# An RWKV-6 block on one core: the last group's recurrence and back part divided by time instead of by channels and sequences

## The chip, the cores and the metric

One core of one Trainium2 chip runs the whole kernel. The metric is the device time of a run in microseconds (us); the time before is the median of three runs, 1524.67 (1521.03 to 1527.92). Engines are called as the profile calls them: PE (matrix products and transposes), PEld (its weight loads), DVE (VectorE), ACT (ScalarE), POOL (GpSimd), SP (issues most DMAs).

## The reference

Input are 32 sequences of 128 tokens with 512 channels (32 heads of 16), a state for each sequence, and the weights of one RWKV-6 layer:

```
xn = ln(x);  sx = token_shift(xn)                       # previous token minus this one
x5 = xn + sx * (maa_stack + tanh((xn + sx*maa_x) @ maa_w1) @ maa_w2)      # five mixes
w = exp(-exp(time_decay + tanh(x5[1] @ decay_w1) @ decay_w2))
r, k, v = x5[3] @ Wr.T, x5[0] @ Wk.T, x5[2] @ Wv.T;  g = silu(x5[4] @ Wg.T)
per sequence and head, token after token, s is 16x16:
    a = k[:, None] * v[None, :];   out = r @ (u * a + s);   s = a + w[:, None] * s
x = x + (groupnorm(out) * g) @ Wo.T
xn2 = ln(x);  xk, xr = two token-shift mixes of xn2
x = x + sigmoid(xr @ ffn_Wr.T) * (relu(xk @ ffn_Wk.T)**2 @ ffn_Wv.T)
```

All is computed in float32.

## The kernel before

**Groups and parts.** The 32 sequences form 8 groups of 4 (512 tokens each). For each group five generators make the instructions: `front_mix` (layer norm, transposes, mixes), `front_proj` (decay, k, r, v), `front_gate` (the gate, parked in DRAM as `dgate`), `prep` (bonus sums and products that make the recurrence step two tokens at a time) and `back` (L810: group norm, gate, output product with `wo`, second layer norm, feed-forward part with `fk`, `fr`, `fv`, store). The recurrence is a row of units that goes through all groups.

**The recurrence.** Partitions are (sequence, head), 128 in all. Tokens are taken in pairs, so a row of time has 64 steps. A group has two passes over the value dimension (`dh`, 8 of 16 columns each), and a pass has 16 units, one for each key row q, and a bonus unit. A unit is:

- ACT: copies the pair decays into a PSUM tile `sc` (L705, two buffers) and the first state column into `a` (L716, two buffers);
- POOL (`rec_pool`): `am = v * k` (L730, 128x1024) and the sum of the two halves of each pair into `a` (L734);
- DVE (`rec_dve`): the scan over time `sc = scan(sc, a)` (L752) and `rm = sc * r` (L754, two buffers);
- PE (`rec_pe`): 8 transposing products that add `rm` into the PSUM tile `acc` (L787, one buffer).

The bonus unit is L761, L764 and L768 on DVE and 8 more products. At the end of a pass ACT copies `acc` into `y` (L801). POOL can be at most two units ahead of the scan, since `a` has two buffers and is freed by the scan.

**The back part.** On `y` of a group: squares on ACT (L829), a sum over each head on DVE (L832), a reciprocal square root in twelve small DVE instructions (L835 to L842), the scaling of `y` (L844); then for each of four channel blocks a PE transpose (L855), gain and bias on ACT (L864), the gate on DVE (L866); the `wo` product (L875) and the residual with a running sum (L884). The second layer norm takes squares on ACT (L354), a small power on POOL (L359) between L357 and L361 on DVE, scaling on ACT (L368), transposes (L394), gain and bias (L384, L895), and two mixes on DVE (L898, L910). Then come the products with `fk` (L408), `fr` (L949) and `fv` (L965), two DVE instructions for the result (L954, L956) and the store (L958). Seven groups do it whole; the last group does it in two streams of two sequences each, both of which begin when the whole recurrence has ended.

**What sets the order.** A planner (`Plan`, with a model of each engine and of the tile buffers) decides while the program is built. Each generator yields operations with an engine, an estimated time, what they read and write and the buffers they take; of those that could start first, it takes the one with the earliest due time. `DUE` holds the due times of each part in units of a group; `last1` and `last2` are the two streams of the last group. The emitted order on each engine is fixed, and each engine works through its own in order.

**Last weights.** `last_weights` (L804) loads `wo`, `fk`, `fr` for the last group into the three weight buffers `wt` as those of group 6 come free, and `fv` when `wo` has been used.

```
            for dh in range(NDH):
                ds = slice(dh * DH, (dh + 1) * DH)
                for q in range(S):
                    (am,) = yield Op(POOL, 2.39, r=[(k, None), (v, None)], w=[(0, None)], alloc=["am"], port=True)
                    nc.gpsimd.tensor_tensor(am.t, v[:, ds, :], k[:, q : q + 1, :].to_broadcast([P, DH, L]), ALU.mult)
```

Of the kernel before, what the change touches and what calls it, by code (L numbers as in the profile page):

```python
# [11 lines left out]
ALU = mybir.AluOpType  # L12
# [36 lines left out]
DUE = {"rec": (0.171, 0.811), "mix": (-4.351, -2.486), "proj": (-6.56, 7.24), "gate": (0.525, 0.545), "prep": (-4.001, 1.375), "back": (-0.209, 3.178), "last1": (-27.722, 1.84), "last2": (7.448, 22.404)}  # L49
# [133 lines left out]
def rwkv6_block(ctx: ExitStack, tc: tile.TileContext, x, prev, s0, vecs, u, maa_w1, maa_w2,  # L183
# [53 lines left out]
    ident = const.tile([P, P], F32, name="ident")  # L237
    mhalf = const.tile([P, GB], F32, name="mhalf")
# [42 lines left out]
    def load_x(g, need=None, bs=range(GB)):  # L281
        b0, b1 = bs[0], bs[-1] + 1
        if g == 0:

            (xt,) = yield Op(SP, 0.4, w=[(0, 0), (0, 1)], alloc=["x"], xfer=2.3)
            nc.sync.dma_start(out=xt[:, 0:2, :], in_=x[0:2].rearrange("b t e -> t b e"))
            yield Op(ACT, 1.4, w=[(xt, 2), (xt, 3)], xfer=2.3)
            nc.scalar.dma_start(out=xt[:, 2:4, :], in_=x[2:4].rearrange("b t e -> t b e"))
            nc.scalar.dma_start(out=vec, in_=vecs)
            nc.scalar.dma_start(out=pv, in_=prev)  # L290
            return xt
        (xt,) = yield Op(SP, 0.4, w=[(0, None)], alloc=["x"], xfer=part(4.5, bs), need=need)
        nc.sync.dma_start(out=xt[:, b0:b1, :], in_=x[g * GB + b0 : g * GB + b1].rearrange("b t e -> t b e"))
        return xt

# [30 lines left out]
    def layernorm_T(g, src, sums, vw, vb, which, use, take, need=None, bs=range(GB)):  # L326
# [35 lines left out]
        for b in bs:  # L362
            if g == 0 and sums is None and b % 2:
# [7 lines left out]
        (xnT,) = yield Op(ACT, 0.25, w=[(0, "p")], alloc=["xnT"], need=need)  # L371
        nc.scalar.copy(xnT[:, :, 0].rearrange("p (e b) -> p e b", b=GB)[:, :, bsl],
                       pv[:, 1 - which, :, g * GB + b0 : g * GB + b0 + nb_])
        late = []

        def evict(e, pt):
            if g == 0 and sums is None:

                yield Op(DVE, 0.69, r=[(pt, None)], w=[(xnT, e)])
                nc.vector.tensor_scalar(xnT[:, e * GB + b0 : e * GB + b0 + nb_, 1 : L + 1], bt(pt[:, cols]),  # L380
                                        col(vw, e), col(vb, e), ALU.mult, ALU.add)
            else:
                yield Op(ACT, part(0.78, bs), r=[(pt, None)], w=[(xnT, e)])
                nc.scalar.activation(xnT[:, e * GB + b0 : e * GB + b0 + nb_, 1 : L + 1], bt(pt[:, cols]), AF.Identity,  # L384
# [16 lines left out]

    def row(xnT, e, shift, bs=range(GB)):

        return xnT[:, e * GB + bs[0] : e * GB + bs[-1] + 1, shift : shift + L]
# [34 lines left out]
    def front_mix(g, d):  # L439
# [8 lines left out]
        def use(xnT, e, pt, tiles):  # L448
# [4 lines left out]
            yield Op(DVE, 0.69, r=[(xnT, e), (xnT, "p"), (pt, None)], w=[(sx, e)])  # L453
# [135 lines left out]
    def prep(g, d):  # L589
# [42 lines left out]
        w01 = yield from pair_decays(w, [w])  # L632
        d.update(st=st, w01=w01)
# [61 lines left out]

    def rec_act(gs):

        for g in gs:
            d = data[g]
            yield Op(ACT, 0.0, need=lambda: "w01" in d and ("v", "all") in d)  # L700
            for dh in range(NDH):
                for q in range(S):
                    sc, = yield Op(ACT, 0.59, r=[(d["w01"], None)], w=[(0, None)], alloc=["sc"])

                    nc.scalar.copy(sc.t, d["w01"][:, q : q + 1, :].to_broadcast([P, DH, T2]))  # L705
# [3 lines left out]
    def rec_state(gs):  # L709
        for g in gs:  # L710
            d = data[g]
            yield Op(ACT, 0.0, need=lambda: "w01" in d and ("v", "all") in d)
            for dh in range(NDH):
                for q in range(S):
                    a, = yield Op(ACT, 0.21, r=[(d["st"], None)], w=[(0, 0)], alloc=["a"])
                    nc.scalar.copy(a[:, :, 0], d["st"][:, q, dh * DH : (dh + 1) * DH])  # L716
                    unit[g, dh, q, "a"] = a
            d["st"].open = False

    def rec_pool(gs):  # L720

        for g in gs:
# [3 lines left out]
            for dh in range(NDH):  # L726
                ds = slice(dh * DH, (dh + 1) * DH)
                for q in range(S):
                    (am,) = yield Op(POOL, 2.39, r=[(k, None), (v, None)], w=[(0, None)], alloc=["am"], port=True)
                    nc.gpsimd.tensor_tensor(am.t, v[:, ds, :], k[:, q : q + 1, :].to_broadcast([P, DH, L]), ALU.mult)  # L730
                    yield Op(POOL, 0.0, need=lambda: (g, dh, q, "a") in unit)
                    a, am2 = unit[g, dh, q, "a"], pair(am.t)
                    yield Op(POOL, 1.03, r=[(am, None)], w=[(a, 1)], port=True, end=[am])
                    nc.gpsimd.tensor_tensor(a[:, :, 1:T2], am2[:, :, 0 : T2 - 1, 0], am2[:, :, 0 : T2 - 1, 1], ALU.add)  # L734
# [3 lines left out]
    def rec_dve(gs):  # L738

        for g in gs:  # L740
# [4 lines left out]
            for dh in range(NDH):  # L745
                ds = slice(dh * DH, (dh + 1) * DH)
                for q in range(S):
# [4 lines left out]
                    nc.vector.tensor_tensor_scan(scf, scf, a.t.rearrange("p d n -> p (d n)"), 0.0, ALU.mult, ALU.add)  # L752
                    (rm,) = yield Op(DVE, 1.21, r=[(sc, None), (r, None)], w=[(0, None)], alloc=["rm"], end=[sc])
                    nc.vector.tensor_tensor(  # L754
                        pair(rm.t), sc.t.unsqueeze(3).to_broadcast([P, DH, T2, 2]),
                        r2[:, q : q + 1, :, :].to_broadcast([P, DH, T2, 2]), ALU.mult)
# [4 lines left out]
                nc.vector.tensor_tensor(rm.t, v[:, ds, :], d["rk"].t.unsqueeze(1).to_broadcast([P, DH, L]), ALU.mult)  # L761
                (am,) = yield Op(DVE, 0.67, r=[(v, None), (d["a10"], None)], w=[(0, None)], alloc=["ps"], port=True)
                bo = am.t.rearrange("p (d n) -> p d n", n=T2)
                nc.vector.tensor_tensor(bo, v2[:, ds, :, 0], d["a10"].t.unsqueeze(1).to_broadcast([P, DH, T2]),  # L764
                                        ALU.mult)
                yield Op(DVE, 0.67, r=[(am, None)], w=[(rm, None)], end=[am])
                rm2 = pair(rm.t)
# [23 lines left out]
    def rec_out(gs):  # L791
        for g in gs:
            d = data[g]
            for dh in range(NDH):
                yield Op(ACT, 0.0, need=lambda: (g, dh, "acc") in unit)
                acc = unit[g, dh, "acc"]
                if dh == 0:
# [6 lines left out]
    def last_weights(W):  # L804

        for name, ap in (("wo", wo), ("fk", fk), ("fr", fr)):
            W[name] = yield from weight(ap, lambda: ("back", "weights") in data[NG - 2])
        W["fv"] = yield from weight(fv, lambda: ("wo", "used") in W)

    def back(g, d, bs=range(GB), W=None):  # L810
# [11 lines left out]
        yield Op(DVE, 0.0, need=lambda: "rec" in d and ("gate", NE - 1) in d)  # L822
        y = d["y"]
        yv = y[:, b0 * H : b1 * H, :]
        n = (b1 - b0) * H
        wot = yield from get("wo", wo, lambda: g < 1 or ("back", "weights") in data[g - 1])
# [199 lines left out]
```

## Time and profile before

The profiled execution took 1523.82 us, with a span of 1522.0 from the first to the last instruction.

| what | value |
|---|---|
| median of three runs | 1524.67 us |
| profiled execution: its time / its span | 1523.82 / 1522.0 us |
| mean granted PE clock | 0.963 |
| PE busy | 1407.3 us (92%) |
| DVE busy | 1264.1 us (83%) |
| POOL busy | 1036.0 us (68%) |
| ACT busy | 652.7 us (43%) |
| DMA moved | 147.04 MB, mean 97 GB/s |

In the profile, busy is the time in which an engine has an instruction under way; `x` behind a tile counts instructions. In a group's line stand the program's names, the shapes, the busy time, the mean duration of one in nanoseconds, and the idle time before them with what ended it. In a timeline each line gives the start, the length and, in brackets, the idle time before it and what ended that. A line of the table by stages gives, for a stretch of the span, each engine's busy time and number of instructions, and last the granted PE clock, the DMA share and GB/s.

### The profile page before, as it was taken

How to read it: one execution, taken by the hardware profiler on the slowest of the kernel's cores; microseconds unless marked ns; L12 is line 12 of the kernel's file. 1: busy time of each engine (PE TensorE's matmuls, PEld its weight loads, DVE VectorE, ACT ScalarE, POOL GpSimd, SP SyncE). 2: the span in 40 equal slices, each digit the busy share in tenths (PEclk: the TensorE clock that was granted, in tenths of full speed). 3: DMA queues.
4: the chain of work that ended last, by engine and by line, in shares of the span. 5: the costliest groups of instructions: out<-in, count | busy, mean ns of one | idle time of the engine just before them, and what ended most of it. 6: DMA issues, size and time to landing. Idle time of an engine off the chain costs nothing.

```text
span 1522.0 us, 16610 instructions
## 1 busy us (share of the span) xinstructions
PE 1407.3 (92%) x5344; PEld 746.5 (49%) x5344; DVE 1264.1 (83%) x1614; ACT 652.7 (43%) x1271; POOL 1036.0 (68%) x642
## 2 busy tenths in 40 slices
PE   5897988889999999999999999999999999689778
PEld 2343454445554555445544555455544555455444
DVE  6539789888998899889988899899988898878732
ACT  3333243324743356423743366423843363344252
POOL 3225884877586959687786959687786959679500
PEclk9897899899999999999999999999999999889989
DMA  6130330424304531244304521244304421400220
GB/s 225 56 87 14 118 103 15 142 82 138 118 24 139 168 102 43 80 143 135 117 31 133 184 86 42 90 143 131 111 32 140 150 98 35 159 28 29 95 71 28
DMA packets 127879, 147.04 MB, mean 97 GB/s; under 512 B 8368, under 2 KB 77616, under 8 KB 126768
## 3 DMA queue, kind: packets, MB, share of 16 engines
q1 hardware_dynamic: 91312, 127.59, 25.4%
q10 hardware_dynamic: 36480, 18.39, 4.2%
q8 instruction: 42, 0.69, 0.2%
q14 instruction: 45, 0.37, 0.1%
HBM read 94.57 MB, written 17.83 MB: 74 GB/s over the span
## 4 chain that ended last, share of the span: by engine, by line
PE 51%; DVE 21%; POOL 18%; issue 5%; ACT 3%; DMA 2%; SPq 0%; POOLq 0%; DVEq 0%; ACTq 0%
PE ps L408 18%; POOL am L730 10%; PE acc L787 8%; PE ps L965 6%; POOL a L734 6%; PE ps L949 6%; PE ps L427 5%; DVE sc L752 4%; DVE rm L754 3%; PE ps L875 2%; PE ps L414 2%; PE ps L465 2%; DVE rk L668 1%; DVE ps L660 1%; POOL mx L488 1%
## 5 line engine op out<-in xcount | busy, mean ns | idle before, releaser
L730 POOL TENSOR_TENSOR am<-v,k 128x1024 f32<-128x1024 f32 x256 | 609.0, 2379 | 34.2 <-DMA r<-blk 15.6
L408 PE MATMUL ps<-mx,wt 128*128 128x512 f32 (+1 forms) x1312 | 585.0, 593 | 17.8 <-DVE mx L456 6.6
L734 POOL TENSOR_TENSOR a<-am 128x504 f32<-128x504 f32 x256 | 286.5, 1119 | 209.4 <-DVE sc L752 183.2
L408 PEld LDWEIGHTS ps<-mx,wt 128*128 128x128 f32 x1312 | 243.8, 194 | 287.4 <-issue 261.9
L752 DVE TENSOR_TENSOR_SCAN sc<-sc,a 128x512 f32<-128x512 f32 x256 | 313.4, 1224 | 35.4 <-POOL a L734 32.3
L754 DVE TENSOR_TENSOR rm<-sc,r 128x1024 f32<-128x1024 f32 x256 | 312.8, 1222 | 32.3 <-PE acc L787 17.1
L787 PE MATMUL acc<-by_head,rm 128*128 128x128 f32 x2176 | 291.5, 284 | 39.1 <-DVE rm L754 37.0
L787 PEld LDWEIGHTS acc<-by_head,rm 128*128 128x128 f32 x2176 | 254.0, 146 | 135.8 <-DVE rm L754 53.8
L705 ACT COPY sc<-w 128x512 f32<-128x512 f32 x256 | 151.2, 591 | 250.6 <-DVE rm L754 225.7
L488 POOL TENSOR_TENSOR mx<-mx,xnT 128x512 f32<-128x512 f32 x94 | 111.6, 1198 | 72.9 <-DVE mx L486 68.7
L716 ACT COPY a<-st 128x8 f32<-128x8 f32 x256 | 51.4, 203 | 153.4 <-DVE sc L752 131.9
L949 PE MATMUL ps<-wt,mx 128*128 128x512 f32 x256 | 115.7, 594 | 0.1
L875 PE MATMUL ps<-wt,mx 128*128 128x512 f32 x256 | 113.3, 600 | 0.2 <-DVE rk L668 0.2
L965 PE MATMUL ps<-wt,ev 128*128 128x512 f32 x224 | 103.2, 604 | 2.7 <-DVE mx L493 2.7
L562 ACT COPY blk<-ps 128x512 f32<-128x512 f32 x96 | 56.0, 583 | 103.8 <-PE ps L408 94.8
L359 POOL TENSOR_TENSOR rstd<-rstd,mhalf 128x4 f32<-128x4 f32 (+1 forms) x17 | 20.2, 1191 | 116.7 <-DVE rstd L357 116.7
L486 DVE SCALAR_TENSOR_TENSOR mx<-ps,vec,sx 128x512 f32<-128x512 f32 x94 | 69.0, 743 | 25.3 <-PE ps L427 25.1
L427 PE MATMUL ps<-tha,w2p 64*128 64x512 f32 x256 | 82.2, 674 | 3.4 <-DVE mx L493 3.4
L875 PEld LDWEIGHTS ps<-wt,mx 128*128 128x128 f32 x256 | 49.1, 194 | 60.9 <-issue 56.4
L491 DVE SCALAR_TENSOR_TENSOR ps<-ps,vec,sx 128x512 f32<-128x512 f32 x66 | 49.6, 752 | 31.7 <-PE ps L427 31.3
L949 PEld LDWEIGHTS ps<-wt,mx 128*128 128x128 f32 x256 | 46.4, 190 | 51.1 <-issue 46.9
L965 PEld LDWEIGHTS ps<-wt,ev 128*128 128x128 f32 x224 | 41.1, 193 | 45.8 <-issue 40.2
(110 smaller groups left out, 1331.4 us busy)
## 6 DMA issues: line engine op xcount, KB each, us to landing
x<-in_x SPq DMA_DIRECT2D x13, 1024.0 KB
wt<-in_wk SPq DMA_DIRECT2D x8, 1024.0 KB
wt<-in_wr SPq DMA_DIRECT2D x8, 1024.0 KB
wt<-in_wg SPq DMA_DIRECT2D x8, 1024.0 KB
dgate<-blk SPq DMA_DIRECT2D x32, 256.0 KB
wt<-in_wo SPq DMA_DIRECT2D x8, 1024.0 KB
wt<-in_fk SPq DMA_DIRECT2D x8, 1024.0 KB
wt<-in_fr SPq DMA_DIRECT2D x8, 1024.0 KB
```

What stands on the lines that cost most here:

```text
L408: nc.tensor.matmul(p, lhsT=w[:, c, e * P : (e + 1) * P], rhs=xin[:, c, cols], start=(c == 0), stop=(c == NE - 1))
L427: nc.tensor.matmul(p.t, lhsT=w[h, :], rhs=t[h, :], start=True, stop=True)
L488: nc.gpsimd.tensor_tensor(bt(x5[:, f, :]), bt(x5[:, f, :]), row(xnT, f, 1), ALU.add)
L705: nc.scalar.copy(sc.t, d["w01"][:, q : q + 1, :].to_broadcast([P, DH, T2]))
L730: nc.gpsimd.tensor_tensor(am.t, v[:, ds, :], k[:, q : q + 1, :].to_broadcast([P, DH, L]), ALU.mult)
L734: nc.gpsimd.tensor_tensor(a[:, :, 1:T2], am2[:, :, 0 : T2 - 1, 0], am2[:, :, 0 : T2 - 1, 1], ALU.add)
L752: nc.vector.tensor_tensor_scan(scf, scf, a.t.rearrange("p d n -> p (d n)"), 0.0, ALU.mult, ALU.add)
L754: nc.vector.tensor_tensor(pair(rm.t), sc.t.unsqueeze(3).to_broadcast([P, DH, T2, 2]), r2[:, q : q + 1, :, :].to_broadcast([P, DH, T2, 2]), ...
L787: nc.tensor.matmul(acc[:, i, :], lhsT=rm[:, i, :], rhs=by_head, is_transpose=True, start=(q == 0 and i % 4 == 0), stop=(q == S), skip_grou ...
L875: nc.tensor.matmul(p.t, lhsT=att[:, c, b * L : (b + 1) * L], rhs=wot[:, c, :], start=(c == 0), stop=(c == NE - 1))
L949: nc.tensor.matmul(p.t, lhsT=xr[:, c, b * L : (b + 1) * L], rhs=frt[:, c, :], start=(c == 0), stop=(c == NE - 1))
L965: nc.tensor.matmul(p2.t, lhsT=kv[:, c, b * L : (b + 1) * L], rhs=fvt[:, c, :], start=(c == 0), stop=(c == NE - 1))
```

## The change

1. **Last group's recurrence by time.** For group 7 the two passes no longer take 8 value columns each over all 64 time steps, but all 16 columns over 32 steps each: first tokens 0 to 63, then 64 to 127 (`passes`, `shaped`). The sizes of the tiles stay. The state after the first half is carried in a tile `st2` (the second `st` buffer): POOL adds the last pair of `am` (a new instruction of 128x16 in each of 16 units), DVE adds the scan's last column times the decay `wdl` (a new instruction of 128x16 in each of 16 units), and ACT starts the second pass's `a` from it. `prep` of group 7 copies the decay column of step 32 into `wdl` and zeroes it.
2. **Back part by time.** `last1` is now tokens 0 to 63 of all four sequences and starts when the first pass has ended; `last2` is tokens 64 to 127. In `y` a half is 64 partitions (its tokens) of 128 rows (sequence and head) of 16, where it was 128 partitions of 64 rows, so the squares, sums, small instructions and scaling of a half have 64 partitions and twice the length. ACT's copy of `acc` to `y` becomes two copies per pass. The second stream needs the first one's `xnT` (token shift across the halves) and waits for its mixes. Loads of `x` and stores of the result take 64 tokens of a sequence each; the gate loads take 64 tokens of four sequences.
3. **Last weights.** `wo`, `fk`, `fr` of the last group go into the free buffers `v`, `r`, `w` of the recurrence, loaded once group 6's recurrence is done, and `fv` into a `wt` buffer when group 6's back part has loaded its own.
4. **Due times.** `back` of group 6 gets its own due times ("penult"), `last1` and `last2` new ones.

```diff
-DUE = {"rec": (0.171, 0.811), ... "last1": (-27.722, 1.84), "last2": (7.448, 22.404)}
+DUE = {"penult": (-0.088, 10.134), "rec": (0.171, 0.811), ... "last1": (-17.026, 23.532), "last2": (5.247, 19.015)}
...
+    wdl = Buf(const.tile([P, S], F32, name="wdl"))
...
+        if len(bs) < GB:
+            (xt,) = yield Op(SP, 1.0, w=[(0, None)], alloc=["x"], xfer=part(4.5, bs), need=need)
+            for o in range(2):
+                nc.sync.dma_start(out=xt[o * L // 2 : (o + 1) * L // 2, b0:b1, :], in_=halves_of(x, g, b0)[o])
+            return xt
...
+        if W is not None and b0:
+            yield Op(ACT, 0.0, need=lambda: "ln2" in W)
+            xnT = W["xnT"]
...
+        if g == NG - 1:
+            yield Op(DVE, 0.25, w=[(w01, None), (wdl, None)])
+            nc.vector.tensor_copy(wdl.t, w01[:, :, T2 // 2])
+            nc.vector.memset(w01[:, :, T2 // 2 : T2 // 2 + 1], 0.0)
+            (d["st2"],) = yield Op(DVE, 0.0, alloc=["st"], need=lambda: "st free" in data[g - 1])
...
+    def passes(g):
+        for i in range(NDH):
+            if g < NG - 1:
+                yield i, slice(i * DH, (i + 1) * DH), slice(0, L), slice(0, T2), DH, T2
+            else:
+                yield i, slice(0, S), slice(i * L // 2, (i + 1) * L // 2), slice(i * T2 // 2, (i + 1) * T2 // 2), S, T2 // 2
+    def shaped(t, nd):
+        f = t.t.rearrange("p d n -> p (d n)")
+        return f.rearrange("p (d n) -> p d n", d=nd)
...
+                    if g == NG - 1 and dh:
+                        yield Op(ACT, 0.0, need=lambda: ("carry", q) in unit)
+                        st = d["st2"]
...
+                    nc.gpsimd.tensor_tensor(amv, v[:, ds, ts], k[:, q : q + 1, ts].to_broadcast([P, nd, 2 * nn]), ALU.mult)
+                    if g == NG - 1 and dh == 0:
+                        yield Op(POOL, 0.25, r=[(am, None)], w=[(d["st2"], q)], port=True)
+                        nc.gpsimd.tensor_tensor(d["st2"][:, q, :], am2[:, :, nn - 1, 0], am2[:, :, nn - 1, 1], ALU.add)
...
+                    if g == NG - 1 and dh == 0:
+                        yield Op(DVE, 0.2, r=[(sc, None)], w=[(d["st2"], q)])
+                        nc.vector.scalar_tensor_tensor(d["st2"][:, q, :], scv[:, :, nn - 1], wdl[:, q : q + 1],
+                                                       d["st2"][:, q, :], ALU.mult, ALU.add)
+                        unit["carry", q] = True
...
+                if g == NG - 1:
+                    for o in range(2):
...
+                        to = d["y"][dh * L // 2 : (dh + 1) * L // 2, :, :].rearrange("p l (d o) -> p o d l", o=2)
+                        nc.scalar.copy(to[:, o, :, :], acc[o * L // 2 : (o + 1) * L // 2, :, :])
+                    d["rec", dh] = True
...
-        for name, ap in (("wo", wo), ("fk", fk), ("fr", fr)):
-            W[name] = yield from weight(ap, lambda: ("back", "weights") in data[NG - 2])
-        W["fv"] = yield from weight(fv, lambda: ("wo", "used") in W)
+        for name, ap, tag in (("wo", wo, "v"), ("fk", fk, "r"), ("fr", fr, "w")):
+            need = lambda: "w01" in data[NG - 1] and "rec" in data[NG - 2]
+            (t,) = yield Op(SP, 0.4, w=[(0, None)], alloc=[tag], xfer=4.5, need=need)
...
+        W["fv"] = yield from weight(fv, lambda: ("back", "weights") in data[NG - 2])
...
-        yield Op(DVE, 0.0, need=lambda: "rec" in d and ("gate", NE - 1) in d)
+        yield Op(DVE, 0.0, need=lambda: (("rec", h) if half else "rec") in d and ("gate", NE - 1) in d)
...
-        (sq,) = yield Op(ACT, part(1.9, bs), r=[(y, 0), (y, 1)], w=[(0, None)], alloc=["ev"])
+        (sq,) = yield Op(ACT, 1.9, r=yr, w=[(0, None)], alloc=["sx" if half else "ev"])
...
-            v0, v1 = DUE[name]
+            v0, v1 = DUE["penult" if name == "back" and g == NG - 2 else name]
```

## The prediction

> **What bounds the kernel now.** I read the table by stages, then the timelines of POOL, DVE and PE from 1290 us on. Group 7's first `am` starts at 1295.09; its two passes end with `a` of their sixteenth units at 1372.2 and 1430.0; PE's last recurrence product ends at 1436.55; the span ends at 1522.0.
>
> ```profile
> 1295.00:1372.00 77.00, 55.04 (x224) 36.69 (x224) 61.20 (x74) 31.30 (x61) 54.89 (x34) 0.82 0.26 92
> 1372.00:1436.00 64.00, 60.93 (x253) 35.59 (x254) 54.98 (x54) 23.44 (x48) 55.53 (x33) 0.97 0.08 29
> 1436.00:1522.00 86.00, 64.85 (x198) 35.96 (x195) 29.94 (x75) 34.10 (x69) 1.40 (x2) 0.90 0.22 77
> ```
>
> Columns: stretch, length, busy time of PE, PEld, DVE, ACT, POOL. In the tail PE has 65 of 86 us: 21 us idle is what the change can win there. In the recurrence no engine is full, but the chain of waits in the second pass is POOL's, one unit in 3.53 us (2.43 from `am` to `a`, 1.10 to the next `am`); DVE follows it. In the first pass POOL waits for DVE, which works off group 6's back part:
>
> ```profile
> 1316.44 2.35 POOL L730 TENSOR_TENSOR am<-v,k 128x1024 f32<-128x1024 f32 x1
> 1325.95 1.03 POOL L734 TENSOR_TENSOR a<-am 128x504 f32<-128x504 f32 x1 [7.16 <-DVE sc L752]
> ...
> 1341.35 2.34 POOL L730 TENSOR_TENSOR am<-v,k 128x1024 f32<-128x1024 f32 x1
> 1352.51 1.02 POOL L359 TENSOR_TENSOR rstd<-rstd,mhalf 128x4 f32<-128x4 f32 x1 [8.81 <-DVE rstd L357]
> ```
>
> The 7.16 us are DVE's normalisation of `y` (L832 to L844, 1315.76 to 1324.6); the 8.81 are four `wo` products in a row with DVE waiting for each. A third thing to see is that a DVE instruction with both inputs in SBUF and a POOL instruction exclude each other:
>
> ```profile
> 1186.53 4.22 DVE L844 TENSOR_TENSOR y<-y,th 128x2048 f32<-128x2048 f32 x1
> ```
> ```profile
> 1186.25 2.36 POOL L730 TENSOR_TENSOR am<-v,k 128x1024 f32<-128x1024 f32 x1
> 1188.68 2.95 POOL L734 TENSOR_TENSOR a<-am 128x504 f32<-128x504 f32 x1
> ```
>
> L844 takes 2.29 alone (at 1322.38); here it waits till `am` ends at 1188.6, and `a` (1.03 alone) then waits for it. L752 and L754, with an operand in PSUM, do not.
>
> **The change, step by step.** I take the changed kernel's order on each engine and put these durations on it.
>
> *Start.* Until 1294 all is as before. The decay column costs DVE 0.27 (a 128x16 memset is 0.07; the copy is bounded by that and by L640's 0.27).
>
> *Pass 1 up to unit 5.* DVE now does the normalisation of group 6 before unit 2's `rm` instead of after it: +1.13 before scan 3, on which `a` of unit 5 waits. Three state additions on DVE come ahead too. No row shows them; a 128x4 of that kind is 0.16 to 0.20 (L361), a 128x64 0.23, so I take 0.2 each (bounds 0.16 to 0.23; an added instruction of an in-order engine is no gain). The shift also makes POOL's `am` of unit 5 start just as the small instructions do, which cost them up to 2.4 us; 0 is the other end, and I take 2.4, as L836's median of 1.16 (0.23 alone) and L844's of 4.22 show the collision is the usual case. Sum 0.27+1.13+0.6+2.4 = 4.4: unit 5's `a` starts at 1330.3 instead of 1325.95.
>
> *Rest of pass 1.* The `wo` products are now interleaved with the recurrence, so the 8.81 and the power (1.0) go from here. What is late next is POOL itself, with its added 128x16: between 0.20 (128x4, L264) and 0.43 (128x128, L313), nearest 0.23, with 0.07 gap 0.30. A unit is 3.83, ten units 38.3: `a` of unit 15 starts at 1368.6, ends 1369.6. DVE's ten units (2.67 each with the addition, plus four L866 of 0.65 and four L884 of 0.75) need 32.3 and fit. So pass 1 ends 2.6 us earlier than before.
>
> *The seam.* Here a wait is added. In the new order the second layer norm of group 6 stands at the seam: DVE issues L357, two bonus instructions, then L361, which needs POOL's power, and POOL has that behind `am, a, am, a, am` of pass 2: 1369.6+0.07+2x3.53+2.43 = 1379.1, power until 1380.1. DVE reaches L361 at some 1374, so it stands 6 us. Behind it wait the last bonus instruction (0.7), the first scan of pass 2, and PE's last product and ACT's copies of `acc`. The scan starts at 1381.1.
>
> *Pass 2 on DVE.* From there DVE is the bound, since the first half's back part lies on it too: 16 scans at 1.33 and 16 `rm` at 1.14 39.5; bonus 2.5; normalisation 8.9 (2.28+4.3+2.29: half the partitions, twice the length, so as in a whole group); group 6's L898 and L910, eight at 0.67, 5.4; of the first half L866 4x0.42, L884 2x0.75, L898 and L910 7x0.48, small ones 0.5: 7.1. Sum 63.4. POOL needs 16x3.53+1.75 = 58.2 and waits. Idle time of DVE: 1.8 for the squares (two copies of `acc` at 1.9 and L829 at 1.9 stand ahead on ACT), 1.5 for the lock against `am` of unit 5 (0 to 2.4), 1.5 for the first `wo` product after PE's idle stretch (one such took 5.14 at 1297.73 against 3.60). The bonus `rm` is ready at 1381.1+63.4+4.8 = 1449.3, PE's last recurrence product ends at 1450.2, 13.6 later than before.
>
> *Tail.* The PE order after it holds more than before, because group 6's products were moved back: 17 full rows (four 128x512 products) at 3.44, 7 halves at 1.72, some 4 us of transposes: 74.5; before, 12, 8 and 5, or 60. To the last transposes: 13x3.44+3x1.72+1.6 = 51.5. This hides the second half's whole chain: copies, squares, sum, L954 and L956, small instructions, scaling 16.4 against 19.0 of PE work ahead of its transposes; the layer norm 5.7 against two rows, 6.9. Then from transposes to the first `fk` row 6.4 (1467.4 to 1473.8 now), three halves 5.2, four rows 13.8, the end 4.4 (1517.6 to 1522.0): 81.3, against 85.4 now. Span 1450.2+81.3 = 1531.5, 9.5 above 1522.0.
>
> *Free by cover.* The weights put 3 MB ahead of `wo`, gates and `x` on SP's queue, and their issue waits for group 6's last bonus (1306.9). The DMA view peaks at 371 GB/s, so 8.5 us, and all 6 MB land by some 1326; L866 wants the gates at 1333. Uncovered, it would cost what they come late, 0 to 5 us. Half loads, gate rows of 256 bytes and half stores are issued ahead or beside PE work; the last store is two issues of 0.4, so 0 to 0.5. Scan, `am` and `rm` over 32 steps instead of 64 keep their size: L754 with broadcast and L761 without both take 1.22, so 0 (bounds 0 and 0.06 each, 3 us in all, from L486's 0.74 against L493's 0.69).
>
> A rule speaks against the second half. The Trainium skill, VectorE: DVE Perf Modes, section "Two Vector instructions with no wait between them", says that an instruction whose operands start in another 32-partition group than the last one's waits until all earlier ones have finished. In this trace scans start 1.14 after an `rm` of 1.22, 0.08 of overlap; the second half works from partition 64, so by the rule some eight switches would cost 0.6 us, and the span would be 1532.1. No run here shows it, and my sum leaves it out.
>
> **The rivals.**
>
> *Faster: the waits swallow it.* DVE had 16 us of idle time in pass 1 and 9 in pass 2. If the collisions and the seam's wait do not come (DVE running later against POOL, so that the power is ready), POOL bounds both passes: `a` of unit 5 at 1325.95, ten units 38.3, pass 2 58.2+1.1, last `rm` and PE 6: 1429.5, span 1511, time 1513. It decides if DVE ends its last unit within 6 us of POOL. Against it: pass 2's 63.4 us of DVE work.
>
> *No change: one of the two comes.* Seam or collisions cost 3 to 4 us instead of 11: PE's recurrence ends near 1441, time 1524.
>
> *Slower still: a tail with holes.* PE has only 3 us idle in my tail. The `x` load of the second half needs group 6's `x` buffer, free after a store that ends 1.7 us too early for comfort; the four `ps` buffers are held by rows waiting for ACT and DVE; a pause brings back the half clock (0.53 at 1445 to 1455 now). 5 to 15 us: 1539 to 1548.
>
> *It does not do what it says.* The emitted order shows the first half's `wo` and first `fk` row inside pass 2, but its remaining 11 rows behind it, as much as group 6 left behind: this is why my tail shrinks by 4 us only.
>
> **Numbers.** The run's time is its span plus 1.82: 1533.3 against 1523.82, +9.5. The median shown is 0.85 above that run, so on its scale 1534.2. What a measurement of this kernel can tell from no change is about 0.5%, or 7.6 us: 1517.0 to 1532.3 is the same. Chances: forecast 0.50 (1526 to 1541), faster 0.15, no change 0.15 (1518 to 1528), holes 0.20. Faster by over 0.5%: most of the first rival, 0.14. Same: the third case, the lower part of the forecast, 0.34. Slower: 0.52. The range, 1514 to 1545, takes in the bounds above and most of the rivals.
>
> **What would show it.** Right: after pass 1 DVE idle some 6 us before L361, released by POOL; POOL waiting for scans in pass 2; PE's last recurrence product near 1450; a tail of 81 us with PE over 90% busy. Wrong: no wait at the seam, the recurrence ending before 1440, or a tail over 86.

## The result, and the profile after

The changed kernel took 1534.78 us (median of 6 runs, 1530.07 to 1536.49), the kernel before 1525.04 beside it: a ratio of 1.0062, with an interval of 1.0042 to 1.0083. A second measurement gave 1535.04 against 1521.70, 1.0097 (1.0081 to 1.0112). The change makes the kernel slower by 10 to 13 us; forecast were 1534.2 us and +9.5.

The profiled execution took 1534.6 us, its span is 1532.8, and its mean clock 0.959. The table by stages, cut about where the first pass, the last recurrence product and the span end (stretch, length, busy time of PE, PEld, DVE, ACT, POOL, then granted clock, DMA share, GB/s):

```profile
1295.00:1372.00 77.00, 52.91 (x224) 34.94 (x224) 67.12 (x88) 24.40 (x51) 60.11 (x49) 0.82 0.42 144
1372.00:1450.00 78.00, 55.17 (x248) 36.81 (x249) 63.91 (x79) 42.99 (x81) 51.01 (x32) 0.81 0.04 14
1450.00:1532.00 82.00, 75.06 (x219) 37.85 (x217) 25.61 (x49) 26.49 (x49) 0.71 (x1) 1.00 0.14 39
```

Against before, the second stage is 14 us longer, with DVE busy for 63.9 us where it was 55.0 and PE for fewer (55.2, was 60.9). The tail is full: PE busy for 75 of 82 us at clock 1.00, where it had 65 of 86. But it is only some 3 us shorter, since the work in it has grown by 10.

**How positions are compared.** The instruction that makes `w01` of group 7 (L650 before, L677 after) has the same DVE order ahead of it in every variant, yet starts between 1288.7 and 1292.7 from execution to execution. So I count from it. Here it starts at 1289.11, before at 1291.84: times of the two profiles that are put side by side below are shifted by 2.7. The two starts, in DVE's timelines of before and of after:

```profile
1291.84 2.29 DVE L650 TENSOR_TENSOR w<-w 128x1008 f32<-128x1008 f32 x1
```
```profile
1289.11 2.29 DVE L677 TENSOR_TENSOR w<-w 128x1008 f32<-128x1008 f32 x1
```

From this start to the end of the last recurrence product it was 144.7 us before and is 161.1 now; the tail behind it was 85.4 and is 82.6. From the same start to the first scan of the second pass it was 89.5 and is 89.2: the first pass and the seam together cost nothing net, and the whole loss of the recurrence lies in the second pass, which took 55.2 us from that scan on and now takes 71.9. That scan before (after's stands below, under the seam):

```profile
1381.36 1.22 DVE L752 TENSOR_TENSOR_SCAN sc<-sc,a 128x512 f32<-128x512 f32 x1
```

**First pass.** What answers to the 7.16 us of POOL's wait, in POOL's timeline:

```profile
1317.54 2.34 POOL L777 TENSOR_TENSOR am<-v,k 128x1024 f32<-128x1024 f32 x1
1319.96 0.22 POOL L782 TENSOR_TENSOR st<-am 128x16 f32<-128x16 f32 x1
1327.87 1.01 POOL L786 TENSOR_TENSOR a<-am 128x496 f32<-128x496 f32 x1 [7.69 <-DVE sc L803]
```

and in DVE's:

```profile
1292.65 2.08 DVE L657 COPY wdl<-w 128x16 f32<-128x16 f32 x1
...
1317.37 0.22 DVE L915 TENSOR_SCALAR th<-th 128x128 f32<-128x128 f32 x1
1317.62 2.35 DVE L916 TENSOR_SCALAR th<-th 128x128 int32<-128x128 int32 x1
```

L916 does the work of L915's size in 2.35 us and ends just when POOL's `am` (1317.54 to 1319.88) has ended; the copy of 128x16 takes 2.08, to 1294.73, while an `am` runs from 1292.36 to 1294.70. This is the exclusion that the prediction reads from L844 and `am`, here with a single input in SBUF. The wait of 8.81 for the power (L359 before) is gone: POOL runs one unit in 3.70 us from here, and `a` of unit 15 starts at 1364.90.

**The seam.** DVE's timeline, where `nb` needs POOL's power (`rstd`), and POOL's, where that power stands behind three `am` of the second pass:

```profile
1370.51 2.83 DVE L822 TENSOR_TENSOR ps<-v,a 128x512 f32<-128x512 f32 x1
1377.64 0.16 DVE L372 SCALAR_TENSOR_TENSOR nb<-mv,rstd 128x4 f32<-128x4 f32 x1 [4.29 <-POOL rstd L370]
1377.71 0.68 DVE L826 TENSOR_TENSOR rm<-rm,ps 128x512 f32<-128x512 f32 x1
1378.31 1.22 DVE L803 TENSOR_TENSOR_SCAN sc<-sc,a 128x512 f32<-128x512 f32 x1
```
```profile
1374.29 2.34 POOL L777 TENSOR_TENSOR am<-v,k 128x1024 f32<-128x1024 f32 x1
1376.58 1.02 POOL L370 TENSOR_TENSOR rstd<-rstd,mhalf 128x4 f32<-128x4 f32 x1
```

**Second pass.** POOL, which set the pace before, now waits: the longest time is that of DVE's normalisation of the first half. DVE in turn waits little. These are POOL's line, and the two longest rows of the table of DVE's waits between the first scan and the last bonus instruction (total, times, longest):

```profile
1401.50 1.01 POOL L786 TENSOR_TENSOR a<-am 128x496 f32<-128x496 f32 x1 [11.31 <-DVE sc L803]
```
```profile
DVE x L969 <- PE ps L960: 3.2, 2, 2.7
DVE th L912 <- ACT sx L909: 2.4, 1, 2.4
```

PE's timeline has the first half's output products, which take 9.03 us here where the second half's take 7.03 (at 1488.18; the granted clock is 0.57 from 1400 to 1410), and the end of the recurrence:

```profile
1404.59 9.03 PE L960 MATMUL ps<-v,mx 128*128 128x512 f32 x16
...
1449.21 1.04 PE L845 MATMUL acc<-by_head,rm 128*128 128x128 f32 x8
```

The collision that the prediction's third and fourth fences show (an earlier group) is the same in the profile after, 4.23 and 2.96 us: L924 and L786 in the line numbers of after.

### The profile page after: what moved, and what is told of

The parts are those of the page before. It is cut to its first block, busy times and chain, and to the rows that moved or that the text cites. A ratio compares the mean times of both kernels' runs of the same rounds, so it can differ in the third digit from the quotient of the medians.

```text
span 1532.8 us, 16660 instructions
## 1 busy us (share of the span) xinstructions
PE 1402.4 (91%) x5360; PEld 744.0 (49%) x5360; DVE 1278.3 (83%) x1632; ACT 658.2 (43%) x1272; POOL 1040.2 (68%) x658
## 4 chain that ended last, share of the span: by engine, by line
PE 55%; DVE 21%; POOL 15%; issue 5%; ACT 3%; DMA 2%; SPq 0%; POOLq 0%; ACTq 0%; DVEq 0%
PE ps L429 20%; PE acc L845 9%; POOL am L777 9%; PE ps L1056 7%; PE ps L1036 7%; PE ps L448 5%; POOL a L786 5%; DVE sc L803 3%; DVE rm L811 3%; PE ps L960 2%; PE ps L435 2%; PE ps L486 2%; DVE rk L695 1%; DVE ps L687 1%; PE ps L410 1%
## 5 line engine op out<-in xcount | busy, mean ns | idle before, releaser
L429 PE MATMUL ps<-mx,wt 128*128 128x512 f32 x1248 | 567.2, 602 | 14.3 <-DVE mx L477 6.6
L786 POOL TENSOR_TENSOR a<-am 128x504 f32<-128x504 f32 (+1 forms) x256 | 285.8, 1116 | 222.2 <-DVE sc L803 195.7
L429 PEld LDWEIGHTS ps<-mx,wt 128*128 128x128 f32 x1248 | 230.3, 193 | 279.5 <-issue 258.8
L762 ACT COPY a<-st 128x8 f32<-128x8 f32 (+1 forms) x256 | 51.7, 205 | 144.3 <-DVE sc L803 126.6
L1036 PE MATMUL ps<-wt,mx 128*128 128x512 f32 x224 | 101.3, 595 | 0.0
L960 PE MATMUL ps<-wt,mx 128*128 128x512 f32 x224 | 98.0, 592 | 0.2 <-DVE rk L695 0.2
L960 PEld LDWEIGHTS ps<-wt,mx 128*128 128x128 f32 x224 | 42.1, 190 | 51.7 <-issue 47.6
L1036 PEld LDWEIGHTS ps<-wt,mx 128*128 128x128 f32 x224 | 40.6, 190 | 45.4 <-issue 41.1
```

Source lines behind the costliest of these rows:

```text
L429: nc.tensor.matmul(p, lhsT=w[:, c, e * P : (e + 1) * P], rhs=xin[:, c, cols], start=(c == 0), stop=(c == NE - 1))
L786: nc.gpsimd.tensor_tensor(shaped(a, nd)[:, :, 1:nn], am2[:, :, 0 : nn - 1, 0], am2[:, :, 0 : nn - 1, 1], ALU.add)
L960: nc.tensor.matmul(p.t, lhsT=att[:, c, b * L : (b + 1) * L], rhs=wot[:, c, :], start=(c == 0), stop=(c == NE - 1))
L1036: nc.tensor.matmul(p.t, lhsT=xr[:, c, b * L : (b + 1) * L], rhs=frt[:, c, :], start=(c == 0), stop=(c == NE - 1))
```

## The experiments

**My theory:** the first half's back part is put on DVE, which then bounds the second pass, so the recurrence ends later by more than the tail gets shorter. **Rivals:** the early loads of the weights delay something; the new due times of group 6 are the cause (its rows were pushed into the tail); the carry of the state is; or the tail is bound by something other than PE's work.

All runs, with the spans of their profiles cut at the end of the last recurrence product and counted from L677's (L650's) start. "Beside" is the median of the kernel before in the same measurement:

| run | time us | beside | ratio (interval) | to the last recurrence product | tail | sum |
|---|---|---|---|---|---|---|
| before | 1525.04 | | | 144.7 | 85.4 | 230.2 |
| after | 1534.78 | 1525.04 | 1.0062 (1.0042 to 1.0083) | 161.1 | 82.6 | 243.7 |
| r1_after | 1535.04 | 1521.70 | 1.0097 (1.0081 to 1.0112) | 161.2 | 82.5 | 243.7 |
| e1_seam | 1533.98 | 1523.56 | 1.0063 (1.0045 to 1.0082) | 157.4 | 83.4 | 240.7 |
| r2_seam | 1533.83 | 1521.70 | 1.0088 (1.0072 to 1.0103) | 159.8 | 82.5 | 242.3 |
| e2_weights | 1521.19 | 1523.56 | 0.998 (0.9966 to 0.9994) | 146.7 | 81.7 | 228.4 |
| r3_weights | 1519.63 | 1521.70 | 0.9989 (0.998 to 0.9999) | 145.9 | 80.8 | 226.6 |
| e3_penult | 1535.72 | 1523.56 | 1.0075 (1.0057 to 1.0092) | 176.2 | 65.2 | 241.4 |
| e5_latefirst | 1538.34 | 1523.56 | 1.0096 (1.0078 to 1.0115) | 144.7 | 101.9 | 246.6 |
| e4_nocarry | 1533.00 | 1525.24 | 1.0065 (1.0049 to 1.0081) | 159.0 | 82.6 | 241.5 |
| e6_nonorm | 1531.91 | 1525.24 | 1.0056 (1.0035 to 1.0077) | 157.3 | 83.7 | 241.0 |
| e7_due | 1527.97 | 1525.24 | 1.0026 (1.0014 to 1.0037) | 160.2 | 74.9 | 235.1 |
| e8_fvshort | 1529.60 | 1525.24 | 1.0029 (1.0017 to 1.0041) | 159.9 | 76.2 | 236.1 |

Up to the end of the recurrence `e8_fvshort` is the changed kernel, since its edit lies behind it. So 161.1, 161.2 and 159.9 us show how far single executions of one program differ there: 1.3 us.

### Does DVE's added work set the end of the recurrence? (e5_latefirst)

```diff
-yield Op(DVE, 0.0, need=lambda: (("rec", h) if half else "rec") in d and ("gate", NE - 1) in d)
+yield Op(DVE, 0.0, need=lambda: (("rec", 1) if half else "rec") in d and ("gate", NE - 1) in d)
```

> The changed kernel with the first half's back part held until the whole recurrence has ended, so that pass 2 carries none of it. Nothing is left out. Theory A: pass 2 loses the normalisation and mixes of the first half on DVE (16 us) and with them the wait for the squares, POOL becomes its bound at 3.5 us a unit, and PE's last recurrence product ends near 1434 to 1438; the tail then holds some 9 us more on PE (one output product of two rows, one half row, transposes) and the start of it is covered by group 6's products: 90 to 95 us. Sum 1526 to 1532: 1 to 7 us faster than the changed kernel. Theory B: the recurrence ends as late as in the changed kernel, and the time grows by the 9 us.

The recurrence ended 16.5 us earlier, after 144.7 us, as long as before the change; in its second pass POOL was the bound again, behind the third unit without a wait and with one unit in 3.52 us:

```profile
1418.77 1.02 POOL L786 TENSOR_TENSOR a<-am 128x496 f32<-128x496 f32 x1
...
1422.29 1.01 POOL L786 TENSOR_TENSOR a<-am 128x496 f32<-128x496 f32 x1
```

That part is confirmed: the first half's back part is what ends the recurrence later. The run takes it off DVE, ACT and PE together, so it does not tell which of them carries it. The tail missed: 101.9 us instead of 90 to 95. The stages, and PE's waits in the tail:

```profile
1372.00:1436.00 64.00, 42.66 (x205) 29.74 (x206) 51.47 (x49) 31.00 (x57) 53.93 (x33) 0.81 0.06 17
1436.50:1538.50 102.00, 89.79 (x265) 45.95 (x263) 40.41 (x82) 39.40 (x72) 1.41 (x2) 0.94 0.16 42
```
```profile
1453.43 0.46 PE L935 MATMUL ps<-ident,y 64*128 64x64 f32 x4 [2.13 <-DVE mx L949]
...
1456.08 9.63 PE L960 MATMUL ps<-v,mx 128*128 128x512 f32 x16 [0.73 <-DVE mx L949]
```

PE has 90 us of work there: what the early first half costs in the recurrence (16.5 us) it gives back in the tail (19.4 us). Without an early first half nothing of the change is left but its costs.

### What in the added work? (e6_nonorm)

```diff
+        if not half or b0:
             nc.vector.tensor_reduce(m2, sqv, AX.X, ALU.add)
 ...
+        if not half or b0:
             nc.vector.tensor_tensor(yv, yv, yy.unsqueeze(2).to_broadcast([nl, n, S]), ALU.mult)
```

The instructions between the two are left out in the same way.

> The changed kernel with the first half's normalisation left out on DVE: the sum over heads, the twelve small instructions and the scaling of y (2.28 + about 4 + 2.3 = 8.6 us in the second pass, and the 2.3 us wait for the squares ahead of them), so the first half's values are not normalised; the squares on ACT stay, and the order of all other instructions is the same. Theory A (in the second pass DVE is the bound, and its added back work is what the recurrence ends later by): the last recurrence product ends 9 to 11 us earlier, near 1440, the tail stays at 82 to 84, and the time falls by 8 to 11 us to 1524 to 1527. Theory B (POOL or PE would be the bound right behind DVE): the recurrence ends 0 to 4 us earlier, and the time is 1530 to 1535. Theory C (the recurrence ends earlier, but the tail grows by as much, since PE has no idle time to fill): 1532 to 1535 with a tail over 90.

Theory A missed: the time fell by 2.9 us, the recurrence ended 3.8 earlier instead of 9 to 11 (4.6 earlier if counted from the first scan of the second pass). DVE's line where the normalisation was:

```profile
1395.30 0.75 DVE L987 SCALAR_TENSOR_TENSOR mx<-xnT,vec,ps 128x512 f32<-128x512 f32 x1 [6.44 <-ACT ps L984]
```

DVE now waits 6.44 us for ACT. At the seam ACT has the two copies of `acc` (1.89 each), the squares (1.91), the units' columns and group 6's second layer norm to do, and DVE's normalisation lay beside them. So the cost at the seam has two carriers, DVE and ACT, one just behind the other; taking away DVE's part shows 3.8 us, while moving all of the first half behind the recurrence (e5_latefirst) shows 16.5. "DVE is the bound" is too simple for the pass's first 20 us. For the rest it is a reading of the profile, where DVE is busy for 43.1 of the 48.4 us from 1400.0 to 1448.4 and POOL for 35.5; no run takes DVE's work alone away there.

### The carry (e4_nocarry)

```diff
-nc.gpsimd.tensor_tensor(d["st2"][:, q, :], am2[:, :, nn - 1, 0], am2[:, :, nn - 1, 1], ALU.add)
-nc.vector.scalar_tensor_tensor(d["st2"][:, q, :], scv[:, :, nn - 1], wdl[:, q : q + 1],
-                               d["st2"][:, q, :], ALU.mult, ALU.add)
-nc.scalar.copy(shaped(a, nd)[:, :, 0], st[:, q, ds])
+nc.scalar.copy(shaped(a, nd)[:, :, 0], d["st"][:, q, ds])
```

> The changed kernel without the carry: POOL's 16 instructions of 128x16 (0.22 each, with their gap 0.29 a unit) and DVE's 16 state additions (0.15 in the pitch) are left out, and the second pass starts from the state that the first one started from, so the second half's values are other ones; the order of all other instructions is the same. Theory A (in the first pass POOL is the bound from unit 5 on): POOL's first pass ends ten units x 0.29 = 2.9 us earlier, with the first five up to 4.6; the first scan of the second pass follows, and the time falls by 2 to 4.6 us, to 1530 to 1533. Theory B (another wait, the seam's for POOL's power or DVE's work in the first pass, takes it up): no change, within 1 us of 1534.8.

In the profile the first scan of the second pass came 2.2 us earlier and the recurrence ended 2.2 us earlier, at the near end of theory A and not far above the 1.3 us by which executions differ. The median is 1.8 us lower, but the ratio to the kernel before beside it, 1.0065, is not lower than after's 1.0062: the times do not show a gain. The carry is at most a small part of the cost.

### The seam (e1_seam, and once more as r2_seam beside r1_after)

```diff
-(nb,) = yield Op(DVE, 0.16, ..., port=True, end=[mv])
+late_nb = (lambda: (NG - 1, 1, 1, "rm") in unit) if g == NG - 2 and sums is not None else None
+(nb,) = yield Op(DVE, 0.16, ..., port=True, end=[mv], need=late_nb)
```

> The changed kernel with one place in the order moved: the DVE instruction of group 6's second layer norm that needs POOL's power is issued after the second unit of pass 2 instead of ahead of the bonus unit's last instruction of pass 1. Nothing is left out. Theory A (the loss is DVE's chain through both passes, the wait at the seam among it, and then a tail filled by PE): the 4.3 us wait ahead of that instruction goes, the first scan of pass 2 comes some 4 to 5 us earlier, PE's last recurrence product ends near 1446 instead of 1450, and the time falls by 4 to 5 us, to some 1530. Theory B (the split by time itself costs it: state additions on POOL, double copies, colder PE): DVE waits for something else instead, and the time stays within 1 us of the changed kernel's.

> The changed kernel once more, as the scale for the two runs beside it: 1534.8 within 1.5 us.

> The kernel of the seam experiment once more, beside the changed kernel on the same chip, since its profile showed the recurrence 3.8 us shorter (counted from the same instruction) and its first times showed nothing. Theory A (the wait of DVE for POOL's power at the seam costs 3 us): 2 to 4 us under the changed kernel's median. Theory B (what the profile showed is the difference between two executions, or is given back in the tail): within 1 us of it.

In both profiles the wait at the seam is gone, and the first scan of the second pass starts 85.8 us after L678 instead of 89.2: 3.4 us are won there. At the end of the recurrence it is 3.8 us in one execution and 1.4 in the other, and the medians are lower by 0.8 and 1.2 only. What differs between the two executions shows in the first half's output products, in PE's timelines of e1_seam and of r2_seam:

```profile
1404.69 7.03 PE L961 MATMUL ps<-v,mx 128*128 128x512 f32 x16
```
```profile
1402.99 9.04 PE L961 MATMUL ps<-v,mx 128*128 128x512 f32 x16
```

In both, PE had stood idle shortly before, waiting for `y` (6.45 and 5.47 us); whether it has its full clock again when these products come differs between executions of one program (9.03 and 9.09 us in after and r1_after). DVE's residual waits for them: twice in r2_seam, 3.2 us in all, and 0.48 in e1_seam. So the seam's wait is real, and by the sums of the profiles it is worth 1 to 3 us, not 4 to 5; by the times it is some 1 us and not clear of their spread, and neither of my two theories was confirmed by them.

### Group 6's place (e3_penult)

```diff
-v0, v1 = DUE["penult" if name == "back" and g == NG - 2 else name]
+v0, v1 = DUE[name]
```

> The changed kernel without its fourth part's entry for group 6: group 6's back part keeps the due times of the other groups, so its products stand in the two passes again instead of behind them. Nothing is left out. Theory A: the tail after PE's last recurrence product holds 10 full rows and 4 halves on PE instead of 17 and 7, and is no longer covered: it becomes the second half's own chain, some 15 us to its transposes, 7 for its output product, 6 for the layer norm, 30 to the end, 59 to 65 in all instead of 82. The recurrence ends later by the DVE work of group 6's result (four times 1.3 us) and by waits for products, near 1452 to 1460. Sum 1512 to 1525, so 5 to 20 us faster than the changed kernel and level with or faster than before. Theory B (the split itself is what costs): no faster than the changed kernel.

The tail came as expected (65.2 us), the recurrence did not: 176.2 us instead of 163 to 171 (the expected 1452 to 1460, counted from L677 of after), and the time did not fall. DVE's waits in the second pass and PE's timeline:

```profile
1391.18 1.22 DVE L811 TENSOR_TENSOR rm<-sc,r 128x1024 f32<-128x1024 f32 x1 [3.03 <-PE acc L845]
1398.97 1.23 DVE L811 TENSOR_TENSOR rm<-sc,r 128x1024 f32<-128x1024 f32 x1 [5.43 <-PE acc L845]
```
```profile
1381.54 8.73 PE L429 MATMUL ps<-mx,wt 128*128 128x512 f32 x16
1390.11 1.04 PE L845 MATMUL acc<-by_head,rm 128*128 128x128 f32 x8
1390.98 3.60 PE L429 MATMUL ps<-mx,wt 128*128 128x512 f32 x8
1394.42 3.60 PE L1036 MATMUL ps<-wt,mx 128*128 128x512 f32 x8
1397.85 1.96 PE L845 MATMUL acc<-by_head,rm 128*128 128x128 f32 x16
```

Two of group 6's rows in a row, the first ones slow, hold up the recurrence's products, these hold both `rm` buffers, and DVE stands. These two waits are 8.5 of the 15.1 us by which the recurrence is longer than after's; 4.1 are there at the first scan of the second pass already, and the rest is not taken apart here. Group 6 in the tail is thus not the cause of the loss: taken out of the tail in this order, it costs as much in the recurrence.

### Only the order (e7_due)

```diff
-"penult": (-0.088, 10.134) ... "last1": (-17.026, 23.532), "last2": (5.247, 19.015)
+"penult": (-0.834, 8.039) ... "last1": (1.831, 15.329), "last2": (9.558, 7.987)
```

> The changed kernel with other due times (group 6's back part -0.834 and 8.039, the first half 1.831 and 15.329, the second 9.558 and 7.987), and nothing else. The emitted order then has all of group 6's rows and, of the first half, two output products ahead of the last recurrence product; behind it lie about 15 rows of products instead of 17 full rows and 7 halves. Theory A (the halves themselves cost only the added back work on DVE in the second pass; it is the order chosen for the rest that leaves PE idle for 47 us during the recurrence and full behind it): the recurrence ends later, 1455 to 1465, the tail is 58 to 68, and the time is 1518 to 1529, within 0.5% of before. Theory B (the recurrence by halves of time costs 10 us in any order): 1532 to 1540.

The time is as theory A has it, 1527.97, but not by the parts I gave: the recurrence ended hardly earlier than after (160.2), and the tail took 74.9 us instead of 58 to 68. Its stage, and the hole that opens it in PE's timeline:

```profile
1452.00:1527.00 75.00, 59.77 (x186) 34.15 (x184) 25.61 (x53) 34.16 (x64) 1.44 (x2) 0.90 0.13 32
```
```profile
1463.27 0.48 PE L410 MATMUL ps<-ident,ev 128*128 128x128 f32 x1 [7.71 <-ACT ev L379]
```

With more of PE's work in the recurrence, too little is left to cover the two halves' chains. Some 7 us of the 10 to 13 (1534.78 against 1527.97) belong to the order chosen; what is left, 0.26% (0.14 to 0.37), is still slower than before.

### Is the tail bound by PE's work? (e8_fvshort)

```diff
-for c in range(NE):
+nc_ = 1 if g == NG - 2 else NE
+for c in range(nc_):
     nc.tensor.matmul(p2.t, lhsT=kv[:, c, b * L : (b + 1) * L], rhs=fvt[:, c, :],
-                     start=(c == 0), stop=(c == NE - 1))
+                     start=(c == 0), stop=(c == nc_ - 1))
```

> The changed kernel with three of the four products of each of group 6's four fv rows left out: 12 products of 128x512, 0.86 us each, 10.3 us of PE work, all behind the last recurrence product; group 6's results are other values, and the order of all other instructions is the same. Theory A (the tail is bound by PE's work): of the two rows ahead of the second half's first transposes (5.2 us) only some 2.6 us come in, since the chain of copies, squares, sum, small instructions and scaling (16.4 us) is then what the transposes wait for, where 19 us of PE work lay ahead; the two rows behind come in whole. The tail falls by 7 to 9 us to about 75, the time to 1526 to 1528. Theory B (the tail is bound by the second half's own chain on ACT, DVE and DMA, and PE's work lies beside it): the tail falls by 0 to 3 us, the time is 1532 to 1535.

The tail fell by 6.3 us to 76.2 and the time by 5.2, between the two theories and nearer to A (7 to 9). Of the 10.3 us of PE work that are left out, 4.0 were not won. PE's lines from the second half's first transposes on show where: a wait of 2.4 us, and some 1.6 us by which the products behind it are slower (L1057 takes 2.07 instead of 1.02, L1036 4.05 instead of 3.60):

```profile
1465.70 0.66 PE L935 MATMUL ps<-ident,y 64*128 64x64 f32 x4 [2.37 <-DVE y L924]
1466.28 2.07 PE L1057 MATMUL ps<-wt,ev 128*128 128x512 f32 x2
1468.15 4.05 PE L1036 MATMUL ps<-wt,mx 128*128 128x512 f32 x8
```

So the tail follows PE's work, and its cover over the second half's chain is only some 3 us thick.

### The weights alone (e2_weights, r3_weights)

Into the kernel before goes part 3 of the change and nothing else:

```diff
-for name, ap in (("wo", wo), ("fk", fk), ("fr", fr)):
-    W[name] = yield from weight(ap, lambda: ("back", "weights") in data[NG - 2])
-W["fv"] = yield from weight(fv, lambda: ("wo", "used") in W)
+for name, ap, tag in (("wo", wo, "v"), ("fk", fk, "r"), ("fr", fr, "w")):
+    need = lambda: "w01" in data[NG - 1] and "rec" in data[NG - 2]
+    (t,) = yield Op(SP, 0.4, w=[(0, None)], alloc=[tag], xfer=4.5, need=need)
 ...
+W["fv"] = yield from weight(fv, lambda: ("back", "weights") in data[NG - 2])
```

> The kernel before with the change's third part alone: the last group's first three weights go into the recurrence's free input buffers early, the fourth into a weight buffer. Nothing is left out. Theory A: within 2 us of before, since the weights were on time before and the 3 MB that now stand ahead of group 6's output weight, gates and input land before these are needed. Theory C (the early 3 MB delay group 6's back part): slower by 3 to 8 us, with DVE waiting for gates or PE for the output weight near 1320 to 1335.

> The kernel before with the last weights in the recurrence's input buffers and nothing else, once more. Theory A (the first measurement's 2 us are real): ratio to before 0.997 to 0.999, upper end under 1. Theory B (they are the spread of the runs): an interval that holds 1.

Both measurements are about 2 us faster than before, with the upper end of the interval under 1. No engine waits for one of the loads in either profile. The tail is shorter by 4 to 5 us (81.7 and 80.8 against 85.4), but the recurrence is longer by 1 to 2 (146.7 and 145.9 against 144.7): with the buffers the planner's order changes too, and POOL waits 5.7 and 5.0 us for the power instead of 8.81, but 3.7 more in the third unit of the second pass. Whether the 2 us come from the loads or from the order is not told apart. This version beats both kernels, by little.

## Why the prediction was right

The time was forecast within 1 us, and the mechanism is the one forecast: the recurrence ends later by more than the tail shrinks. Some terms were mis-sized, and nearly offset each other. Times of after are shifted by 2.7 us here, to stand on the scale of before's profile.

- **Start and pass 1 up to unit 5.** Forecast: `a` of unit 5 at 1330.3. Measured: 1330.6. The agreement is partly luck. The decay copy was costed at 0.27 and took 2.08, because it met `am`. Against that, the collision of the small instructions was put at 2.4 and was 2.1 on L916, while L835, which took 0.81 before, ran in 0.22 (L915); a state addition took 0.23, of which 0.15 lies in the pitch (the distance from one start to the next).
- **Rest of pass 1.** Forecast: unit 3.83, `a` of unit 15 at 1368.6. Measured: 3.70 and 1367.6. POOL's 128x16 took 0.22, and the next instruction started 0.05 before its end.
- **Seam.** Forecast: power until 1380.1, scan at 1381.1, DVE waiting 6 us. Measured: 1380.3, 1381.0; the profile shows 4.29 us of idle time, since L822, a bonus instruction with both inputs in SBUF, took 2.83 instead of 0.69 in the meantime. The position was right; without the wait only 1 to 3 us are won (e1_seam, r2_seam).
- **Pass 2.** This term of the sum was mis-sized most. Forecast: 63.4 us of work and 4.8 of idle time from the first scan to the bonus `rm`, 68.2. Measured: 61.4 busy and 8.7 idle, 70.1. The wait for the squares was 2.4 (1.8 forecast), that for the slowed `wo` products 3.2 (1.5), short waits for PE and ACT that I had left out 1.5, and the other 1.6 are gaps too short for the table of waits. The last product ended 1.8 us after the bonus `rm` (0.9 forecast), so the recurrence ended at 1453.0 on this scale, 2.8 later than forecast. And DVE was not alone: by e6_nonorm ACT stands only some 4 us behind it at the seam.
- **Tail.** Forecast: 81.3 with PE over 90% busy. Measured: 82.6 and 75.1 of 82 (92%) at clock 1.00. The start of 1467.4 that the sum gives the stretch of 6.4 us stands in no row of before; the transposes start at 1467.85, so that term should have been 6.0. e8_fvshort confirms PE as the tail's bound, e5_latefirst that the first half's rows belong to its sum.
- **Free by cover.** Right for the weights: in e2_weights and r3_weights no engine waits for them, and the times are 2 us lower. The second half's gate rows came 2.89 us late for DVE (at 1477.93), beside PE work.
- **Sum.** On this scale the recurrence took 2.8 and the tail 1.3 us more than forecast, and the span is 13.5 above before's instead of 9.5. The measured medians, 9.7 and 13.3 us apart in two measurements, lie on both sides; that the first one agrees to 1 us is partly the spread of the executions, not the accuracy of the terms.
- **Rivals.** "Faster" fell because pass 2 did become DVE's and ACT's. "One of the two" fell because collisions and seam both came; the seam alone is worth only 1 to 3 us. "Does not do what it says" was right as far as it went: 75 us of products lie behind the recurrence. "Holes" did not come in this order, but they did in e7_due (7.71 us) and, smaller, in e5_latefirst (up to 2.13).

**The rule on quadrants.** The Trainium skill, VectorE: DVE Perf Modes, section "Two Vector instructions with no wait between them", agrees with the one pair of rows that tests it here. DVE's timeline, the scaling of the first half (partitions 0 to 63) and of the second (64 to 127), each with the instruction behind it:

```profile
1393.67 2.28 DVE L924 TENSOR_TENSOR y<-y,th 64x2048 f32<-64x2048 f32 x1
1395.88 1.39 DVE L983 SCALAR_TENSOR_TENSOR mx<-xnT,vec,ps 128x512 f32<-128x512 f32 x2
...
1463.93 2.29 DVE L924 TENSOR_TENSOR y<-y,th 64x2048 f32<-64x2048 f32 x1
1466.25 0.70 DVE L1041 SCALAR_TENSOR_TENSOR ps<-th,ps 128x512 f32<-128x512 f32 x1
```

Behind the first the next starts 0.07 us before its end; behind the second, which works from partition 64, 0.03 after it: 0.1 for a switch, about the 0.08 that the prediction took. But the second half's switches all lie in the tail, where DVE waits for PE (5.62 us at 1473.29), so the 0.6 us was rightly left out, if for another reason.

## What to carry to other kernels

Work that is taken out of a tail has to be priced in the stage where it goes, on every engine it uses: here 16.5 us of recurrence bought 19.4 us of tail against doing the first half late, and that late tail was 16.5 us longer than before's. Filling PE's 21 idle us in the tail won only 3 us of tail and nothing of the total, because the rows that fill them came out of the stage ahead: PE's total from 1295 us on is 181 us before and 183 after. Before an operation is removed to show that its engine is the bound, look which engine stands just behind it; the one that shows after the removal was part of the price.

## What the runs showed of the hardware

- A DVE copy of 128x16 (one input, in SBUF) took 2.08 us beside POOL's `am`, and an integer instruction of 128x128 took 2.35 where its neighbours took 0.22 and 0.26; the state additions, with an input in PSUM, took 0.22 to 0.24 throughout. I had priced the copy as if only two inputs in SBUF collide. The Trainium skill, SBUF — State Buffer, section "SBUF: two separate sides", says that a DVE instruction in a two-port mode takes the shared ports exclusively too; these two rows agree with it, at 1.8 and 2.1 us (that they ran in such a mode, no row shows).
- One and the same program had its two rows of output products in 7.03 us in one execution and in 9.04 in another, after the same wait of PE for `y` (6.45 and 5.47 us). The granted clock was 0.59 and 0.50 in a stretch of 20 us before, and 0.90 and 0.62 in the 12 us from there on. So 2 us of PE time can be won or lost here with no change to the program. The Trainium skill, TensorE: Matmul & The Clock Gate, section "Part 1: The HAM clock gate (the "warmup" mystery)", says that the gate's window runs freely and the number of slow products differs from run to run; this pair agrees.
- The start of one instruction with the same order ahead of it lay between 1288.7 and 1292.7 us in the 13 profiled executions: single profiles of this kernel can't be compared to better than that without such a common point.
